# Layer 0 of a four-layer graph network: batches of 16 graphs, nodes packed into tiles by group

## Chip, cores and metric

One core of one Trainium2 chip. The metric is the time of one execution on the device, in microseconds (us), as the median of several runs.

## The reference, cut to what matters

128 graphs of 64 nodes with 256 features go through four layers, each with a residual and a layernorm. Layer 0 works on five groups of nodes (25, 9, 7, 6 and 6 of the first 25 nodes). Each group is two graph convolutions with its own weights, 256 to 512 to 256 features:

```python
GROUPS = [list(range(25)), [0,...,8], [0, 9,...,14], [6, 7, 8, 12, 13, 14], [3, 4, 5, 9, 10, 11]]
for g, idx in enumerate(GROUPS):
    x_g, adj_g = x[:, idx, :], adj[:, idx][:, :, idx]
    h     = relu(norm(adj_g) @ (x_g @ W1[g]) + b1[g])
    out_g = relu(norm(adj_g) @ (h @ W2[g]) + b2[g])
    fused[:, idx, :] += softmax(fusion_w)[g] * out_g
x = layernorm(x + fused)
# layer 1: a graph convolution; layer 2: a polynomial of the adjacency
# layer 3: five rounds of messages into a GRU: most of the matmuls, untouched by the change
```

Everything is float32.

## The kernel before

A chunk is 8 graphs, four pairs of 128 nodes. `back(c)` is layer 3 of chunk c; `front(c + 1)`, layers 0 to 2 of the next chunk, is laid between its steps (a step is what lies between two `yield`s), so that one has matmuls for TensorE while the other waits. Layer 0 puts four graphs' 25 nodes into a tile of 100 rows, two tiles per chunk, and keeps that shape for all five groups: nodes out of a group are zeros.

```python
NT = 2                      # layer-0 tiles of a chunk: four graphs, their first 25 nodes each
R = 4 * NJ                  # 100 rows
def front(c):
    # ... adjacency of the groups (A), transposed (AT); adjacency of the pairs
    # ... ag0 = first aggregation (pa), [features, nodes]
    for g in range(NG):
        hg = work.tile([128, 4, NT * R], F32, name="hg", bufs=2)
        if g:
            nc.gpsimd.memset(hg, 0.0)
        for e in range(4):                                  # ph: W1, only the group's nodes
            p = spread_like(psum("ph"), g)
            for k in range(2):
                nc.tensor.matmul(p, W1[:, g, k, e * 128 : (e + 1) * 128], part(ag0[:, k, g, :], g), ...)
            nc.scalar.activation(part(hg[:, e, :], g), p, AF.Relu, bias=b1[...])
        for t in range(NT):                                 # ps: W2, both full tiles for every group
            for e in range(4):
                nc.tensor.matmul(ps[:, t, :], hg[:, e, t * R : (t + 1) * R], W2[:, g, e, :], ...)
        nc.scalar.copy(s2, ps)
        yield
        for t in range(NT):                                 # po: second aggregation, nodes on partitions
            nc.tensor.matmul(po[:, t, :], AT[:, t, g, :], s2[:, t, :], start=True, stop=True)
        nc.vector.tensor_add(z, po, b2s[...])               # then relu, scale, fused += z
    for t in range(NT):                                     # pse: to the pairs' tiles
        for h in range(2):
            nc.tensor.matmul(p[:, h, :], sel[:, h, :], fused[:, t, :], start=True, stop=True)
        nc.vector.tensor_add(xt[...], p, xt[...])
    layernorm(xt)
    yield
    # ... layers 1 and 2, each ending in a layernorm on VectorE with a power on GpSimd
...
interleave(front(0), fold())
for c in range(NCH):
    if c + 1 < NCH:
        interleave(back(c), front(c + 1))
    else:
        interleave(back(c))
```

## Time and profile before

| | before |
|---|---|
| median of four runs | 2947.6 us (2946.25 to 2948.17) |
| profiled span | 2944.2 us |
| TensorE busy | 2784.7 us, 10712 instructions |
| start, until layer 3 of chunk 0 begins | 149.2 us |
| one chunk in the steady part | 177.4 us |
| last chunk | 134.4 us |

A change is judged by what it does to the start, to a steady chunk, and to the end. In a line of the timeline the columns are start, duration, engine, source line, operation, output and inputs by name, shapes (of a matmul: the stationary operand as rows*columns, then the moving one), count, and in brackets the idle time ahead with what ended it. `pT` is transposes, `pa`/`ph`/`ps`/`po`/`pse` are layer 0's stages (`pa` and `pT` serve other layers too), `pd` the projections of layers 1 and 2, `pn`/`pr`/`pz`/`pi` the GRU's gates and `pm` its messages. The distance from one group's start to the next, divided by its number of instructions, is called the pitch.

### The profile page before, as it was taken

The numbers are of one execution on the slowest core, as the hardware profiler recorded it, in microseconds if no ns is written. First come the engines' busy times: TensorE is split into PE (matmuls) and PEld (weight loads), VectorE is DVE, ScalarE is ACT, GpSimd is POOL, SyncE is SP. The second block draws the span as 40 slices with busy tenths as digits, with TensorE's granted clock in tenths as the row PEclk, the third lists the DMA queues.
The fourth block names the chain that finished last, engine by engine and source line by source line (L and its number), as shares of the span: only waits on it lengthen the run. The fifth ranks groups of instructions, "written<-read, shape, count | busy, mean of one in ns | idle before, by whom it ended". The sixth has DMA issues, their size and how long they took to land.

```text
span 2944.2 us, 27152 instructions
## 1 busy us (share of the span) xinstructions
PE 2784.7 (95%) x10712; PEld 1683.7 (57%) x10712; DVE 1197.2 (41%) x2503; ACT 813.1 (28%) x1443; POOL 182.5 (6%) x178
## 2 busy tenths in 40 slices
PE   4799999999999999999999999999999999999998
PEld 3656565565656656565565656556565565656644
DVE  3433425354352533525244352443525344252433
ACT  0132232322323222232322323223232222223222
POOL 2000100000010000100000000000100000000000
PEclk9899999999999999999999999999999999999999
DMA  5000000000000000000000000000000000000000
GB/s 170 2 4 2 18 1 13 7 2 18 1 17 3 2 18 1 20 0 7 13 2 18 0 17 4 2 18 1 17 3 2 17 1 15 1 8 0 1 7 8
DMA packets 38549, 34.01 MB, mean 12 GB/s; under 512 B 15082, under 2 KB 35762, under 8 KB 38422
## 3 DMA queue, kind: packets, MB, share of 16 engines
q1 hardware_dynamic: 34686, 23.69, 2.7%
q0 software_dynamic: 1504, 5.51, 0.6%
q10 hardware_dynamic: 2232, 3.08, 0.4%
q8 instruction: 85, 1.39, 0.2%
q14 instruction: 42, 0.34, 0.0%
HBM read 23.88 MB, written 8.39 MB: 11 GB/s over the span
## 4 chain that ended last, share of the span: by engine, by line
PE 79%; issue 9%; DVE 8%; POOL 2%; DMA 1%; ACT 1%; ACTq 0%; POOLq 0%; DVEq 0%; SPq 0%
PE ps L317 9%; PE pr L431 8%; PE pz L417 8%; PE pi L431 8%; PE pz L431 8%; PE pn L417 7%; PE pr L417 7%; PE ph L310 5%; PE pm L424 4%; PE po L325 2%; PE pa L226 2%; PE pa L294 2%; PE pT L453 2%; PE pd L369 2%; DVE st L192 1%
## 5 line engine op out<-in xcount | busy, mean ns | idle before, releaser
L436 DVE SCALAR_TENSOR_TENSOR r<-pn,bhh,r 128x512 f32<-128x512 f32 x160 | 120.1, 750 | 1094.4 <-ACT r L435 1094.4
L431 PE MATMUL pr<-agg,V 128*128 128x512 f32 x640 | 307.5, 603 | 0.0
L431 PE MATMUL pz<-agg,V 128*128 128x512 f32 x640 | 300.7, 592 | 0.0
L431 PE MATMUL pi<-agg,V 128*128 128x512 f32 x640 | 300.7, 592 | 0.0
L317 PE MATMUL ps<-W,hg 128*100 128x256 f32 x1280 | 292.7, 382 | 0.0
L435 ACT ACTIVATE r<-pr,brz 128x512 f32<-128x512 f32 x160 | 109.9, 687 | 610.8 <-PE pr L431 610.8
L417 PE MATMUL pn<-hn,WHH 128*128 128x512 f32 x512 | 253.2, 596 | 0.0
L417 PE MATMUL pr<-hn,WHH 128*128 128x512 f32 x512 | 243.6, 592 | 0.0
L317 PEld LDWEIGHTS ps<-W,hg 128*100 128x100 f32 x1280 | 210.1, 168 | 55.4
L417 PE MATMUL pz<-hn,WHH 128*128 128x512 f32 x512 | 240.6, 592 | 0.0
L428 ACT COPY agg<-pm 128x512 f32<-128x512 f32 x160 | 93.8, 586 | 494.8 <-PE pm L424 494.8
L431 PEld LDWEIGHTS pi<-agg,V 128*128 128x128 f32 x640 | 121.6, 190 | 153.1 <-issue 153.1
L431 PEld LDWEIGHTS pz<-agg,V 128*128 128x128 f32 x640 | 121.6, 190 | 153.1 <-issue 153.1
L439 ACT ACTIVATE n<-r,bih 128x512 f32<-128x512 f32 x160 | 115.5, 722 | 291.4 <-DVE r L437 291.4
L310 PEld LDWEIGHTS ph<-ag,W 128*128 128x128 f32 x1280 | 173.2, 191 | 26.4 <-issue 21.5
L431 PEld LDWEIGHTS pr<-agg,V 128*128 128x128 f32 x640 | 108.4, 189 | 124.1 <-issue 76.5
L310 PE MATMUL ph<-ag,W 128*128 128x48 f32 (+3 forms) x1280 | 170.9, 282 | 0.0
L417 PEld LDWEIGHTS pr<-hn,WHH 128*128 128x128 f32 x512 | 97.1, 190 | 122.6 <-issue 117.8
L417 PEld LDWEIGHTS pz<-hn,WHH 128*128 128x128 f32 x512 | 97.2, 190 | 116.1 <-issue 115.4
L197 POOL TENSOR_TENSOR rs<-ve,mhalf 128x4 f32<-128x4 f32 x64 | 64.4, 1007 | 1385.0 <-DVE ve L195 1344.5
L424 PEld LDWEIGHTS pm<-A,h 128*128 128x128 f32 x1024 | 124.4, 192 | 30.6 <-issue 30.6
L313 ACT ACTIVATE hg<-ph,b 128x48 f32<-128x48 f32 (+3 forms) x320 | 107.2, 347 | 95.2 <-PE ph L310 83.5
(109 smaller groups left out, 3264.9 us busy)
## 6 DMA issues: line engine op xcount, KB each, us to landing
xt<-in_x_dram SPq DMA_DIRECT2D x16, 512.0 KB
out_dram<-xt SPq DMA_DIRECT2D x16, 512.0 KB
x<-in_x_dram SPq DMA_DIRECT2D x128, 25.0 KB
W<-in_w_dram POOLq DMA_DIRECT2D x5, 512.0 KB, 8.1
W<-in_w_dram ACTq DMA_DIRECT2D x5, 512.0 KB
a<-in_adj_dram SPq DMA_DIRECT2D x128, 2.4 KB
a<-in_adj_dram SPq DMA_DIRECT2D x16, 128.0 KB
wl<-in_wlT_dram POOLq DMA_DIRECT2D x5, 256.0 KB, 5.5
```

What stands on the lines that cost most here:

```text
L197: nc.gpsimd.tensor_tensor(rs, ve, mhalf[:, :NP], ALU.pow)
L226: nc.tensor.matmul(p[:, q * 128 : (q + 1) * 128], src[:, q, k * 128 : (k + 1) * 128], m[:, q, :], start=True, stop=True)
L310: nc.tensor.matmul(p, W1[:, g, k, e * 128 : (e + 1) * 128], part(ag0[:, k, g, :], g), start=k == 0, stop=k == 1)
L313: nc.scalar.activation(part(hg[:, e, :], g), p, AF.Relu, bias=b1[:, g * 4 + e : g * 4 + e + 1])
L317: nc.tensor.matmul(ps[:, t, :], hg[:, e, t * R : (t + 1) * R], W2[:, g, e, :], start=e == 0, stop=e == 3)
L417: nc.tensor.matmul(p, WHH[:, k, q * 128 : (q + 1) * 128], hT[:, k, :], start=k == 0, stop=last and k == 1)
L424: nc.tensor.matmul(p[:, q * 128 : (q + 1) * 128], h[:, q, k * 128 : (k + 1) * 128], A01[:, q, :], start=True, stop=True,)
L428: nc.scalar.copy(agg[:, k, :], p)
L431: nc.tensor.matmul(p, V[:, l, k, q * 128 : (q + 1) * 128], agg[:, k, :], start=first and k == 0, stop=k == 1)
L435: nc.scalar.activation(r, pr, AF.Sigmoid, bias=brz[:, j : j + 1])
L436: nc.vector.scalar_tensor_tensor(r, pn, bhh[:, 4 + j : 5 + j], r, op0=ALU.add, op1=ALU.mult)
L439: nc.scalar.activation(n, r, AF.Tanh, bias=bih[:, 4 + j : 5 + j])
```

## The change

Its intent: no matmuls on zero rows. Layer 0 now takes 16 graphs at a time and packs each group's nodes alone into tiles: 4 tiles of 100 rows, 2 of 72, one of 112 and two of 96, nine per 16 graphs in place of twenty. Each packed tile is loaded directly. The second aggregation comes out with features on partitions, so that groups can be added by strided views along the free dimension, and `pse` becomes plain transposes. The 16 graphs' layer 0 is laid beside two chunks: ten steps at the end of an even chunk, the others at the beginning of the odd one. The core of the diff:

```diff
+SB = 16
+TILES = [(0, 4 * i, 4) for i in range(4)] + [(1, 8 * i, 8) for i in range(2)] + [(g, 0, SB) for g in (2, 3, 4)]
 ...
-            hg = work.tile([128, 4, NT * R], F32, name="hg", bufs=2)
-            if g:
-                nc.gpsimd.memset(hg, 0.0)
+            hg = work.tile([128, 4, w], F32, name="hg0" if g == 0 else "hg", bufs=1 if g == 0 else 2)
 ...
-            for t in range(NT):
-                nc.tensor.matmul(po[:, t, :], AT[:, t, g, :], s2[:, t, :], start=True, stop=True)
-            nc.vector.tensor_add(z, po, b2s[:, None, g * D : (g + 1) * D].to_broadcast([R, NT, D]))
+            for k in range(2):
+                for u, t in enumerate(ts):
+                    nc.tensor.matmul(p[:, ...], s2[u][:, k * 128 : (k + 1) * 128], AT[:r, t, :r], ...)
+                nc.scalar.activation(F[...] if g == 0 else z[...], p, AF.Relu, bias=gb2[...], scale=gw[...])
+            if g:
+                for f, n in RUNS[g]:
+                    nc.vector.tensor_add(F[:, :, :, f : f + n], F[:, :, :, f : f + n], z[...])
 ...
-                nc.tensor.matmul(p[:, h, :], sel[:, h, :], fused[:, t, :], start=True, stop=True)
+                    nc.tensor.transpose(p[:, h, k * 128 : (k + 1) * 128], F[:, k, b : b + 2, :]..., ident)
 ...
-    interleave(front(0), fold())
+    interleave(front0(0), fold())
+    interleave(front(0))
     for c in range(NCH):
-            interleave(back(c), front(c + 1))
+        if c % 2 == 0:
+            beside = both(front(c + 1), take(half, 10) if s < NS else ())   # half = front0(s), s = c // 2 + 1
+        else:
+            beside = both(half, front(c + 1)) if s < NS else ()
+        interleave(back(c), iter(beside))
```

Cut: the loads, the block masks, and buffers that shrank to make room.

## The prediction

> **What bounds the kernel now.** The page comes first, for its shares and its slices. Then the timeline of TensorE over a steady stretch of 200 us, its first 155 us and its last 210 us, and the whole chain of work for one chunk.
>
> ```profile
> PE 2784.7 (95%) x10712; PEld 1683.7 (57%) x10712; DVE 1197.2 (41%) x2503; ACT 813.1 (28%) x1443; POOL 182.5 (6%) x178
> ...
> PE   4799999999999999999999999999999999999998
> ...
> 40.88 1.91 PE L258 MATMUL pT<-ident,A 100*100 100x100 f32 x10 [40.88 <-DVE A L252]
> ...
> 126.13 3.62 PE L369 MATMUL pd<-L1W,ag 128*128 128x256 f32 x16
> 136.09 3.75 PE L226 MATMUL pa<-poly,xt 128*128 128x128 f32 x16 [6.34 <-DVE xt L199]
> 139.63 3.79 PE L385 MATMUL pd<-L2W,ag 128*128 128x256 f32 x16
> 149.19 2.10 PE L403 MATMUL pT<-ident,xt 128*128 128x128 f32 x8 [5.77 <-DVE xt L199]
> ...
> 1561.54 1.04 PE L453 MATMUL pT<-ident,hn 128*128 128x128 f32 x8
> 1567.65 2.10 PE L403 MATMUL pT<-ident,xt 128*128 128x128 f32 x8 [5.07 <-DVE xt L199]
> 1569.54 0.63 PE L424 MATMUL pm<-A,xt 128*128 128x128 f32 x2
> 1569.97 3.62 PE L417 MATMUL pn<-hT,WHH 128*128 128x512 f32 x4
> 1573.38 1.98 PE L417 MATMUL pr<-hT,WHH 128*128 128x512 f32 x4
> ...
> 1612.04 2.87 PE L310 MATMUL ph<-ag,W 128*128 128x200 f32 x16
> 1614.75 3.62 PE L317 MATMUL ps<-W,hg 128*100 128x256 f32 x16
> 1618.20 1.88 PE L417 MATMUL pn<-hn,WHH 128*128 128x512 f32 x4
> ...
> 1629.37 1.90 PE L310 MATMUL ph<-ag,W 128*128 128x72 f32 x16
> 1631.11 3.64 PE L317 MATMUL ps<-W,hg 128*100 128x256 f32 x16
> ...
> 1745.14 2.10 PE L403 MATMUL pT<-ident,xt 128*128 128x128 f32 x8 [5.07 <-DVE xt L199]
> ```
>
> TensorE is the bound. Between 1573 and 1745 us its groups start one at the end of the other, with one gap of 0.55 us. The only regular hole is at the boundary of chunks: `pT` of the next chunk (L403) waits 5.07 us for the layernorm of layer 2. It costs more than that: after it the four `pn` take 3.41 us to the start of `pr` instead of 1.72, and the eight `pT` 1.89 instead of 0.87. From the end of the last gate (`pz`, 1558.09) to 1573.38 are 15.29 us for 7.13 us of matmuls at full pace, so a boundary loses 8.2 us.
>
> The time of before adds up: the start until the first L403 at 149.19 us, 15 chunks of 177.4 us (to L403 at 2809.84), and a last chunk of 134.4 us without anything beside it; together 2944. The measured median is 3.4 us over the span.
>
> Starts of successive groups, not mean durations, give the price of a matmul. A float32 matmul is two instructions (640 of them for 320 calls on L431), a transpose one. One instruction costs 1.72/4 = 430 ns at 512 moving columns, 3.45/16 = 216 ns at 256, 2.71/16 = 169 ns at 200, 1.78/16 = 111 ns at 128, and still 109 ns at 72. So it is about (larger of moving and stationary columns)/1.2 + 2.5 ns. The ten 100x100 transposes take 0.86 us, 86 ns each, which fits.
>
> **What the Trainium skill says.** TensorE: Matmul & The Clock Gate, section "LDWEIGHTS (loading the stationary operand)": a load lasts by its columns, P/1.2 ns, whatever its rows. The trace agrees (109 ns floor with 128 stationary columns, 86 with 100), and it is why 48 or 72 moving columns cost what 128 do. Same page, section "Back-to-back issue gap": N/2.4 + 2.5 ns for an isolated matmul. Here float32 instructions take N/1.2 + 2.5; the measurement decides. Same page, "Part 1: The HAM clock gate": an idle window of about 3.4 us halves the clock, as long a busy one restores it. The trace agrees: the 5.07 us hole is followed by some 3 us of lost pace, the holes under 1 us by none. Trainium Kernel Development and Optimization, section "Performance Expectations": matmul busy time says little since matmuls overlap; here a group's mean duration (592 ns) indeed exceeds its pitch (430).
>
> **The change, part by part.** *Matmuls of layer 0, for 16 graphs.* Before, one chunk of 8: transposes 0.86; `pa` 8 x 419 ns = 3.35; `ph` 2.71 + 1.74 + 1.78 + 2 x 1.70 = 9.6 (groups 1 to 4 all at the floor); `ps` 80 x 216 ns = 17.3, all five groups on two full tiles of 100 rows though most rows are zero; `po` 20 x 216 ns = 4.3; `pse` 8 x 216 ns = 1.75. Sum 37.2, or 74.4 us for 16 graphs.
>
> After, the nine packed tiles (4 of 100 rows, 2 of 72, one of 112, 2 of 96), with the same pitch rule: transposes 9 x 96 ns = 0.9; `pa` 36 x 111 ns = 4.0; `ph` 16 x 336 (400 columns) + 16 x 122 (144) + 48 x 109 ns = 12.6; `ps` 72 x 216 ns = 15.6, for nine tiles in place of twenty; `po`, now features by nodes, 36 x 109 ns = 3.9; group sum 16 transposes x 109 ns = 1.7. Sum 38.6 us. Saved 35.8 us per 16 graphs, 286 us for all eight. The dropped zero memsets on GpSimd and the dropped bias additions on VectorE (687 ns each) lie beside TensorE and give nothing.
>
> *Boundaries of chunks.* The order of instructions of the changed kernel shows two kinds. After an even chunk, layers 1 and 2 of the next chunk were done in steps 1 to 7 of 17, and L0 work fills the end: no hole. After an odd chunk they take steps 11 to 17: after the last gate come only `pd` of layer 1, the last `pT` of layer 3, then `pa`, `pd` of layer 2 and the next chunk's transposes, each behind a chain on VectorE and GpSimd. That run stands alone in the start of before: `pd` at 126.13 to L403 at 149.19, 23.1 us, with holes of 6.34 and 5.77 us. Add 2.9 us of slow clock afterwards, subtract 9.55 us of full-pace work (3.45 + 0.87 + 1.78 + 3.45): 16.5 us lost. Two boundaries of before lost 16.4, so for the steady part the pair is even: half the holes, each twice as long. For the whole: before 15 x 8.2 = 123, after 7 x 16.5 = 116.
>
> *Small waits.* From the end of the last gate of a round to its `hn` transposed are 2.5 to 2.9 us (2.49 at 2836.32 in the last chunk). Before, long `ph` and `ps` groups covered that in most rounds; now the filler between rounds is often 1.7 us plus 0.44. I take six gaps of 0.4 us, 2.4 us per pair against 1.1.
>
> *Start.* The direct loads of the packed tiles take 30 issues in place of 16, plus two more large loads ahead of the constants. Before, one issue per 1.2 us (the 27th, `bhh`, at 33.45, landed 39.3, and the first transposes waited behind it in VectorE's order). `bhh` is now 43rd: about 16 later, first transposes near 57. The front of 16 graphs instead of 8 adds 1.5 us of matmuls and similar waits (72 us until the group sum, 71 before), then 37 us as before: first L403 at about 167.
>
> *Sum.* Steady work of a chunk outside layer 0 is 130.5 us (177.4 - 37.2 - 8.2 - 0.55, less 1.0 for switches between groups). A pair: 2 x 130.5 + 38.6 + 2 x 1.0 + 16.5 + 2.4 = 320.5. Total: 167 + 7 x 320.5 + 135 (chunk 14, with layers 1 and 2 of the last but no layer 0) + 131.5 (the last, without a cold start) = 2677, and 3.4 outside the span: 2680 us.
>
> **Rivals.** *The waits eat it.* If VectorE, in order and with GpSimd's powers (1.98 us each) in its way, delays the recurrent chain in each of the ten rounds of a pair by 1 us more, and odd boundaries lose 25 us, the sum is 2680 + 8 x 10 + 7 x 8.5 = 2820. Against it: VectorE is 41% busy and loses work. For it: layer-0 scaling with its wait on a power now sits between two rounds. *Only the even boundaries count.* If the odd boundary is no worse than one of before, the time is 2680 - 7 x 8.3 = 2622. For this I see little: the static order puts `pa` and `pd` after the last gate. *The saving is fiction.* If matmuls with 96 to 112 moving columns paid load and stream one after the other (109 + 90 ns), the 120 such instructions (`pa`, `po`, three of `ph`) would add 11 us per 16 graphs, 2770. Against it: 72 columns at 109 ns now. *Loads bind.* Many pieces of 4 to 12 bytes could make the packed tiles late; they are queued a chunk ahead and DMA is at 0 to 1 tenths after the start, so I give it 20 us at most, in the start.
>
> **Range and chances.** Matmul counts are exact and their pitch is measured; a 3% error of the saving is 9 us. The odd boundaries are known to 3 us each (21), the small waits to 2 us per pair (16), the start to 12. Together about 30, with more room above: 2640 to 2730. Faster by over 2% means under 2889, which only several failures at once would miss: 0.97; same 0.02, slower 0.01.
>
> **What would show it.** `ps` at 576 instructions in place of 1280, pitch 216 ns; `po` near 109 ns; `ph` at 400 columns near 336. No hole at even boundaries, at odd ones two of 5 to 7 us, one ahead of `pa` and one ahead of the next chunk's first transposes (L403 of before). Pairs of 320 us. The first of those transposes at 167 us. It is wrong if TensorE's gaps between rounds exceed 1 us, or a pair's length is off by over 8 us.

## The result, and the profile after

2669.3 us (median of four, 2668.16 to 2670.44) against 2947.6: ratio 0.9058, 95% interval 0.9045 to 0.9071. A ratio here is the mean time of one kernel's fast runs over that of the other's of the same rounds, so not quite the ratio of the medians. The prediction was 2680 with 2640 to 2730.

The page of the changed kernel, busy times and TensorE's slices:

```profile
PE 2491.1 (93%) x9408; PEld 1461.6 (55%) x9408; DVE 1077.2 (40%) x2394; ACT 712.9 (27%) x1219; POOL 108.2 (4%) x108
...
PE   2879999899989999899998999989999999989998
```

TensorE lost 294 us of busy time, more than the 276 us by which the span fell, and its slices now show eights between the nines: holes that were spread over every chunk stand together. TensorE's timeline of the changed kernel shows where, at the end of an even chunk and then of an odd one:

```profile
1271.42 1.93 PE L332 MATMUL po<-AT,s 100*128 100x100 f32 x16
1273.19 1.35 PE L500 MATMUL pT<-ident,hn 128*128 128x128 f32 x8
...
1276.34 3.62 PE L319 MATMUL ps<-W,hg 128*72 128x256 f32 x16
1279.79 1.04 PE L450 MATMUL pT<-ident,xt 128*128 128x128 f32 x8
...
1416.14 3.62 PE L416 MATMUL pd<-L1W,ag 128*128 128x256 f32 x16
1419.59 1.04 PE L500 MATMUL pT<-ident,hn 128*128 128x128 f32 x8
1426.04 3.75 PE L236 MATMUL pa<-poly,xt 128*128 128x128 f32 x16 [5.41 <-DVE xt L226]
1429.59 4.75 PE L432 MATMUL pd<-L2W,ag 128*128 128x256 f32 x16
1440.55 2.09 PE L450 MATMUL pT<-ident,xt 128*128 128x128 f32 x8 [6.21 <-DVE xt L226]
1442.43 1.92 PE L358 MATMUL pse<-ident,fusedT 128*128 128x128 f32 x8
1444.14 2.58 PE L464 MATMUL pn<-hT,WHH 128*128 128x512 f32 x4
1446.56 1.88 PE L464 MATMUL pr<-hT,WHH 128*128 128x512 f32 x4
```

At 1279.79 the next chunk's first transposes (L450, the place of L403 before) follow a `ps` without a hole. At the odd boundary there are two holes, each behind a layernorm (L226). From `pd` at 1416.14 to `pr` at 1446.56 are 30.42 us, for 13.0 us of work at full pace (3.45 + 0.87 + 1.78 + 3.45 + 0.87 + 0.87 + 1.72): 17.4 us lost. In the pair before this one the same stretch took 28.43 us, 15.4 lost.

Where the 276 us of the two spans come from:

| stretch | before | after | saved |
|---|---|---|---|
| start, until the first transposes of layer 3 | 149.2 | 164.25 | -15.1 |
| chunks 0 to 13 | 14 x 177.4 = 2483.6 | 7 pairs of 319.07 = 2233.5 | 250.1 |
| chunk 14 | 177.4 | 137.5 | 39.9 |
| last chunk | 134.4 | 132.9 | 1.5 |

A pair saved 2 x 177.4 - 319.07 = 35.7 us.

### The profile page after: what moved, and what is told of

Same layout as the page of the kernel before. It is cut to its first block, busy times and chain, and to the rows that moved or that the text cites. A ratio compares the mean times of both kernels' runs of the same rounds, so it can differ in the third digit from the quotient of the medians.

```text
span 2668.1 us, 23799 instructions
## 1 busy us (share of the span) xinstructions
PE 2491.1 (93%) x9408; PEld 1461.6 (55%) x9408; DVE 1077.2 (40%) x2394; ACT 712.9 (27%) x1219; POOL 108.2 (4%) x108
## 4 chain that ended last, share of the span: by engine, by line
PE 89%; DVE 5%; DMA 2%; ACT 1%; issue 1%; SPq 1%; POOL 1%; POOLq 0%; DVEq 0%; ACTq 0%
PE pr L478 11%; PE pz L478 10%; PE pi L478 10%; PE pz L464 10%; PE pn L464 10%; PE pr L464 10%; PE pm L471 5%; PE ph L305 4%; PE ps L319 3%; PE pa L236 3%; PE pT L500 2%; PE pd L416 2%; PE pd L432 2%; DMA xg<-in_x_dram 1%; PE pp L407 1%; PE po L332 1%
## 5 line engine op out<-in xcount | busy, mean ns | idle before, releaser
L464 PE MATMUL pn<-hn,WHH 128*128 128x512 f32 x512 | 247.8, 595 | 0.0
L478 PEld LDWEIGHTS pr<-agg,V 128*128 128x128 f32 x640 | 108.4, 189 | 124.2 <-issue 76.5
L319 PE MATMUL ps<-W,hg 128*100 128x256 f32 (+3 forms) x576 | 130.9, 379 | 0.0
L490 DVE TENSOR_TENSOR d<-hn,n 128x512 f32<-128x512 f32 x128 | 88.6, 692 | 100.8 <-ACT n L486 100.8
L491 DVE TENSOR_TENSOR d<-d,zg 128x512 f32<-128x512 f32 x160 | 110.5, 691 | 35.9 <-ACT zg L488 35.7
L471 PE MATMUL pm<-A,h 128*128 128x128 f32 x1024 | 124.6, 275 | 0.0
L484 DVE TENSOR_TENSOR r<-pi,r 128x512 f32<-128x512 f32 x160 | 110.7, 692 | 34.5 <-PE pi L478 34.3
```

The source lines that it names most:

```text
L319: nc.tensor.matmul(p[:r, h, :], hg[:, e, TOFF[t] - o : TOFF[t] - o + r], W2[:, g, e, :], start=e == 0, stop=e == 3,)
L464: nc.tensor.matmul(p, WHH[:, k, q * 128 : (q + 1) * 128], hT[:, k, :], start=k == 0, stop=last and k == 1)
L471: nc.tensor.matmul(p[:, q * 128 : (q + 1) * 128], h[:, q, k * 128 : (k + 1) * 128], A01[:, q, :], start=True, stop=True,)
L478: nc.tensor.matmul(p, V[:, l, k, q * 128 : (q + 1) * 128], agg[:, k, :], start=first and k == 0, stop=k == 1)
L484: nc.vector.tensor_add(r, pi, r)
L490: nc.vector.tensor_sub(d, hT[:, j, :], n)
```

## Experiments

The theory: TensorE's work in layer 0 lies wholly on the path, so each instruction less is worth its pitch; boundaries cost what their chains leave uncovered, twice as much at half as many places. Rivals: the relief of VectorE, ScalarE and GpSimd made the gain; the boundary holes are worth nothing in themselves; the turned orientation is a saving of its own. Nine kernels were run; eight gave the right result, one is wrong. The kernel before ran beside each of them with medians of 2947.2 to 2947.7 us, so that medians may be compared. The diffs are shortened, in places to pseudocode.

### 1. Double one stage of layer 0

```diff
-                    for e in range(4):
+                    for e in (0, 1, 2, 3, 0, 1, 2, 3):   # ps, in the changed kernel
```

> The changed kernel with every ps matmul (hidden layer to second weight matrix) done twice, the second round overwriting the first: 72 float32 matmuls = 144 instructions more per 16 graphs, nothing else on any engine; the result stays right. Theory (TensorE is the bound and layer 0's instructions lie on its path at 216 ns per pair of matmul instructions as counted in the prediction, 72 x 216 ns = 15.6 us per 16 graphs): 8 x 15.6 = 124 us more, about 2793 us (2775 to 2805). Rival (the gain of the change came from the lighter VectorE, ScalarE and GpSimd, and TensorE has slack in layer 0): less than 40 us more.

Measured: 2792.1 us (2791.09 to 2792.78), ratio to before 0.9475 (0.946 to 0.9489). That is 122.8 us over the changed kernel, where 124 were expected. The page and the group of `ps` with 100 rows, whose count doubled:

```profile
PE 2614.2 (94%) x9984; PEld 1557.9 (56%) x9984; DVE 1077.3 (39%) x2394; ACT 711.5 (25%) x1219; POOL 108.3 (4%) x108
...
L319 PE MATMUL ps<-W,hg 128*100 128x256 f32 x512 | 111.8, 379 | 0.0
```

The expectation calls the 72 additions matmuls; they are 36 matmuls of two instructions each, and its sum of 72 x 216 ns stands. Nothing else moved: VectorE's busy time is 1077.3 for 1077.2 us. 576 instructions more cost 122.8 us, 213 ns each. So a `ps` instruction is worth its pitch, and 704 fewer of them (1280 to 576) are worth some 152 us of the 278.

### 2. Give the other engines their old load back

```diff
+            if g:
+                for _ in range(3):
+                    nc.gpsimd.memset(hg, 0.0)
 ...  # after the activations of ph
+            for _ in range(2 if g == 0 else 4):
+                nc.vector.tensor_reduce(dv, hg, AX.XY, ALU.add)
+            for e in range(4):
+                for _ in range(2):
+                    nc.scalar.activation(da, hg[:, e, :96], AF.Relu)
```

> The changed kernel with dummy work on the other engines in layer 0, about as much as the change took away: per group 2 or 4 reductions on VectorE over the hidden tile, 8 small activations on ScalarE, 3 zero memsets of the hidden tile on GpSimd ahead of its use; TensorE's instructions and their order are the same, the result stays right. The change took 120 us from VectorE, 100 from ScalarE, 74 from GpSimd. Theory (all of it lay beside TensorE): 2669 to 2685 us with the busy times back near those of before. Rival (this relief was the gain): towards 2900.

Measured: 2668.2 us (2667.24 to 2669.98), 1.1 us under the changed kernel, with 111 us more on VectorE, 76 on ScalarE and 45 on GpSimd. Its page:

```profile
PE 2488.9 (93%) x9408; PEld 1459.9 (55%) x9408; DVE 1188.1 (45%) x2538; ACT 789.0 (30%) x1539; POOL 153.2 (6%) x204
```

VectorE got back 92% of what it had lost, the two others 76% and 61%. The time did not move, so a load of about that size beside layer 0 costs nothing, and the dropped memsets and bias additions gave nothing, as the prediction had it. (The dummy reductions and activations stand in their engines' order, but nothing reads them; only the memsets are ahead of work that TensorE waits for.)

### 3. Turn the second aggregation back

```diff
-                for u, t in enumerate(ts):      # 18 matmuls, [features, nodes], 72 to 112 columns moving
-                    nc.tensor.matmul(p[:, ...], s2[u][:, k * 128 : (k + 1) * 128], AT[:r, t, :r], ...)
+                for h in range(n):              # 9 matmuls, [nodes, features], 256 columns moving
+                    nc.tensor.matmul(p[:r, h, :], AT[:r, ts[u + h], :r], s2[u + h], ...)
```

> The changed kernel with the second aggregation turned back to nodes on partitions (the adjacency stationary, 256 feature columns moving): 9 float32 matmuls of 256 columns in place of 18 of 72 to 112 per 16 graphs; the result is wrong on purpose, because the group sum and the transposes after it are left as they are. Theory (a matmul instruction costs the larger of its moving and stationary columns, so 18 x 216 ns = 3.9 us against 36 x 109 ns = 3.9 us): 2664 to 2675, the same as the changed kernel. Rival (features on partitions is itself a saving on TensorE): 15 us or more slower.

Measured: 2669.4 us (2668.14 to 2670.09) against 2669.3; the result was wrong. Half the instructions at twice the length: the orientation is no saving on TensorE. Its use is that the group sum becomes strided additions.

### 4. Fill the boundaries of the kernel before

```diff
-    interleave(front(0), fold())
+    interleave(front_a(0), fold())              # front_a: layer 0, front_b: layers 1 and 2
+    interleave(front_b(0), front_a(1))
     for c in range(NCH):
-            interleave(back(c), front(c + 1))
+        interleave(back(c), both(front_b(c + 1), front_a(c + 2)))
```

> The kernel before with layer 0 done one chunk further ahead: beside chunk c stand layers 1 and 2 of chunk c+1 and then layer 0 of chunk c+2, so the chain behind the last layernorm has TensorE work beside it at each boundary; the same instructions in all. Theory (a boundary of before loses 8.1 to 8.2 us because nothing else is left to run): 15 x 8.1 = 122 us less, about 2825 us (2800 to 2840), no hole ahead of the first pT of layer 3 over 1 us. Rival (the holes are only the place where a slack shows that some other engine sets): the hole moves elsewhere and the time stays within 20 us of 2947.

Measured: 2870.7 us (2869.27 to 2877.41), ratio 0.9746 (0.9731 to 0.9761): 76.5 us less, not 122. TensorE's timeline at a boundary of this version shows what stayed:

```profile
1563.43 1.97 PE L314 MATMUL pse<-fused,sel 100*128 100x256 f32 x8 [2.87 <-DVE fused L310]
1565.23 1.04 PE L458 MATMUL pT<-ident,hn 128*128 128x128 f32 x8
1566.11 1.04 PE L408 MATMUL pT<-ident,xt 128*128 128x128 f32 x8
```

The 5.07 us hole ahead of the transposes (here L408) is gone, and a new one of 2.87 us stands a little earlier: layer 0 now ends there, and `pse` waits for the sum of the last group. Part of the wait changed its name. The boundary shown is one of the cheapest: behind the same hole the eight `pse` took from 1.96 to 3.75 us from chunk to chunk, and in one of the slowest the granted clock was 0.50 (350 to 353 us). So the experiment was repeated with `pse` and its layernorm moved to the next chunk.

```diff
+    def front_x(c):     # pse, residual and layernorm of layer 0
-        interleave(back(c), both(front_b(c + 1), front_a(c + 2)))
+        interleave(back(c), both(front_x(c + 1), front_b(c + 1), front_a(c + 2)))
```

> As the first filled version of before, but the selection matmuls pse and the layernorm of layer 0 are put off to the start of the next chunk, so that nothing at the end of a chunk waits for the group sum on VectorE. The first version took 2870.7 us and kept a hole of 2.87 us ahead of pse at each chunk's end. Theory (a boundary of before loses 8.1 us, of which 5.2 went with the first version and 2.87 stayed in that hole): 15 x 2.87 = 43 us less, about 2828 us (2815 to 2840), no hole over 1 us in the steady part. Rival (the remaining loss is something else at the boundary and the hole moves on): 2860 to 2870.

Measured: 2806.6 us (2806.57 to 2807.57), ratio 0.9522 (0.9509 to 0.9535). The boundary:

```profile
1520.01 1.11 PE L303 MATMUL po<-s,AT 100*100 100x256 f32 x4
1520.95 1.04 PE L413 MATMUL pT<-ident,xt 128*128 128x128 f32 x8
1522.22 1.98 PE L427 MATMUL pn<-hT,WHH 128*128 128x512 f32 x4 [0.24 <-ACT hT L414]
```

A steady chunk takes 169.26 us (1182.44 to 1520.95 are two of them) in place of 177.4: a boundary cost 8.14 us, which agrees with the prediction's 8.2. 15 x 8.14 = 122. The kernel gained 141; most of the other 19 us came in the start. There layer 0 of chunk 1 now fills the holes of chunk 0's chains: the first transposes of layer 3 are at 166.91, with 35.7 us of chunk 1's layer 0 already done (all but `pse`); less those, that is 131.2, against 149.2 before. The time is 21 us under the expected 2828 and outside its range. The profiles show two terms that the expectation had left out: the start gained 9 us more than in the first version (177.43 less 37.4 there), and a steady chunk fell by 4.4 us (173.7 to 169.3) and not by 2.87, since the slow clock behind the hole went too. (The profiled run of the first version was 6.7 us over its median, so the 4.4 is somewhat too large.)

### 5. Fill the boundaries of the changed kernel

```diff
-        if c % 2 == 0:   beside = front(c + 1), then ten steps of layer 0 of batch c // 2 + 1
-        else:            beside = the other steps, then front(c + 1)
+        if c % 2:        beside = front_x(c + 1), front_y(c + 1), then front_x(c + 2) and ten steps of layer 0 of batch c // 2 + 2
+        else:            beside = front_y(c + 1), then the other steps   # chunk 0: the whole of batch 1
```

`front_x` is here the group sum's transposes with the layernorm of layer 0, `front_y` is layers 1 and 2.

> The changed kernel with its layer-0 batch done half a pair earlier, so that 16 steps of layer-0 work stand beside the chains at the end of both chunks of a pair; the same instructions. Theory (each odd boundary loses 16.5 us by its two holes and the slow clock, each even one nothing): 7 x 16.5 = 115 us less, about 2554 us (2540 to 2580), with no hole of 5 to 7 us from chunk 1 on. Rival (the odd boundary's chain costs no more than one of before, 8.2 us): about 2612. Rival (the gain of the change came from elsewhere and the holes only move): 2640 to 2670.

Measured: 2566.1 us (2565.3 to 2567.06), ratio 0.8708 (0.8695 to 0.8721): 103 us under the changed kernel, by order alone. TensorE's timeline at both kinds of boundary:

```profile
1248.04 1.09 PE L454 MATMUL pT<-ident,xt 128*128 128x128 f32 x8 [0.30 <-ACT z L336]
...
1402.94 3.62 PE L319 MATMUL ps<-W,hg 128*72 128x256 f32 x16
1406.40 1.04 PE L454 MATMUL pT<-ident,xt 128*128 128x128 f32 x8
```

A pair takes 303.98 us (1102.42 to 1406.40), 15.1 less than the 319.07 of the changed kernel; the rule said 16.5. The rival that an odd boundary costs no more than one of before would have given 2612 and is out.

Now two kernels without boundary holes can be compared, which shows the matmuls alone. Layer 0's groups, from start to start in the timelines: 37.4 us for 8 graphs in the filled kernel before (transposes 0.86, `pa` 3.36, `ph` 9.6, `ps` 17.4, `po` 4.5, `pse` 1.7), 39.0 us for 16 in the filled changed one (0.9, 4.0, 12.6, 15.5, 4.3, 1.7). The prediction had 37.2 and 38.6. Per pair of chunks: 2 x 169.26 - 303.98 = 34.5 us of time saved, where 35.8 were predicted.

### 6. Packing or batch

Packed tiles, but 8 graphs at a time (six tiles per 8 graphs), with boundaries and start filled by the same order:

```diff
-SB = 16
+SB = 8
-TILES = [(0, 4 * i, 4) for i in range(4)] + [(1, 8 * i, 8) for i in range(2)] + [(g, 0, SB) for g in (2, 3, 4)]
+TILES = [(0, 4 * i, 4) for i in range(2)] + [(g, 0, SB) for g in (1, 2, 3, 4)]
```

> Packed tiles as in the changed kernel, but in batches of 8 graphs (six tiles per 8 graphs: 2 of group 0 and one of each other), with the chains at the ends of chunks filled; it splits the gain between the packing and the batch of 16. Layer 0 per 8 graphs by the prediction's rule: 6 transposes 0.6, 24 pa 2.7, ph 16 x 169 and 64 x 109 ns = 9.7, ps 48 x 216 = 10.4, 24 po 2.6, 8 transposes 0.9: 26.9 us, against 37.2 in the kernel before and 19.3 in the changed one. Theory: (37.2 - 26.9) x 16 = 165 us under the fully filled before (about 2828) = 2663, and 7.6 x 16 = 122 us over the filled changed kernel (2566) = 2688; so 2660 to 2690. Rival (packing is all, the batch of 16 is worth little): about 2570. Rival (the batch is all): about 2820.

Measured: 2715.6 us (2712.22 to 2717.97), ratio 0.9212 (0.9199 to 0.9224). Both rivals are out, but it lies 26 to 56 us above what I expected. A steady chunk takes 163.12 us; 169.26 - 10.3 = 158.96 was expected, 4.2 less. TensorE's timeline at the end of a chunk, and the stretches around it (stretch, its length, then busy time of TensorE, weight loads, VectorE, ScalarE and GpSimd, granted clock, DMA share, GB/s):

```profile
1622.85 1.93 PE L318 MATMUL ps<-W,hg 128*48 128x256 f32 x8
1628.55 3.42 PE L318 MATMUL ps<-W,hg 128*48 128x256 f32 x8
1632.43 0.64 PE L331 MATMUL po<-AT,s 48*128 48x48 f32 x4 [0.46 <-ACT s L323]
```

```profile
1625.00:1628.00 3.00, 2.74 (x24) 2.45 (x23) 2.59 (x11) 1.39 (x5) 0.00 (x0) 1.00 0.00 0
1628.00:1630.00 2.00, 2.00 (x10) 1.25 (x10) 1.63 (x9) 0.67 (x3) 0.19 (x1) 0.70 0.00 0
1630.00:1633.00 3.00, 2.54 (x9) 1.13 (x7) 1.38 (x4) 0.48 (x2) 0.82 (x1) 0.63 0.00 0
```

From start to start and at full clock, layer 0 sums to 28.7 us for 8 graphs, not 26.9; that its groups of four to eight short instructions change often is my reading, and no run isolated it. At a chunk's end `ph` and then `po` wait for ScalarE, 0.26 us (at 1626.64) and 0.46, 0.72 together. And in seven of the thirteen chunks from 324.61 to 2445.18 the clock fell, as in the second line: the same eight `ps` took 3.0 to 3.6 us and not 1.93. In three of the thirteen it fell at another place, behind layer 0's `pa`. The shortest chunks, with neither, take 161.82 us, so the slow clock is worth some 1.3 us per chunk in the mean. That is 3.8 of the 4.2 us; the other 0.4 I did not take apart.

### 7. The start

In the changed kernel's trace VectorE reads `fw` at 49.21, after 1.63 us of waiting, and the first packed transposes start at 52.82. The small constants were put at the head of another queue:

```diff
+    b2 = const(..., nc.scalar); bih = const(bihT, ..., nc.scalar); bhh = const(bhhT, ..., nc.scalar)
+    fw = spread(fusion_w, NG, "fw", eng=nc.scalar); cw = spread(conv_w, 4, "cw", eng=nc.scalar)
     b1 = const(b1T, [128, NG * 4], "b1", nc.scalar)
```

> The changed kernel with the five small constants that VectorE's first operations wait for (b2, bih, bhh, fw, cw) issued from ScalarE's queue ahead of b1 and W1, in place of behind the packed tiles' loads on SyncE's. Theory (the first packed transposes, at 52.8 us, wait for fw through VectorE's order, landed about 49.2): the first transposes move to 45 to 48 us, and the time falls by 4 to 8 us, to about 2663. Rival (the packed tiles themselves are late): no change within 1 us.

Measured: 2669.6 us (2667.89 to 2670.74), ratio 0.9056 (0.9044 to 0.9069), nothing gained. The first half of the theory held, the second did not. TensorE's and then VectorE's timeline of this version:

```profile
46.39 1.90 PE L279 MATMUL pT<-ident,A 112*112 112x112 f32 x9 [46.39 <-DVE A L259]
48.08 1.94 PE L197 MATMUL pf<-ih,wl 128*128 128x256 f32 x4
51.40 6.87 PE L197 MATMUL pf<-ih,wl 128*128 128x256 f32 x20 [1.37 <-DVE AT L280]
```

```profile
50.39 0.42 DVE L375 TENSOR_REDUCE rsum<-a 128x4 f32<-128x256 f32 x1 [3.01 <-DMA a<-in_adj_dram]
50.73 0.61 DVE L280 TENSOR_TENSOR AT<-pT,d0o 112x448 f32<-112x448 f32 x1
```

The transposes came 6.4 us earlier, but the next operation in VectorE's order was a sum over a later adjacency tile (L375) whose load had not landed. VectorE waited 3.01 us for it while the finished transposes stood behind it. TensorE then waits for VectorE's copies of the folded weights (`pf`) three times, 0.78, 2.27 and 1.02 us, where the changed kernel has one wait of 2.31. At the first `ps` the lead of 6.4 us has become a lag of 1.0 (96.02 against 94.98), and the first `pT` of layer 3 starts at 164.41 against 164.25. The Trainium skill, TensorE: Matmul & The Clock Gate, section "Architectural detail: the array is 16× 32×32, not 1× 128×128", says that VectorE's queue is strictly in order; these lines agree.

The last run filled the start as it had been filled in experiment 4:

```diff
-    interleave(front_y(0), front_x(1))
+    interleave(front_y(0), with_first(front_x(1), front0(1), 10))   # ten steps of batch 1's layer 0
```

> The changed kernel with filled boundaries, and the first ten steps of the second batch's layer 0 put beside layers 1 and 2 of chunk 0 in the start, as chunk 1's layer 0 stood there in the second filled version of before. In the filled changed kernel's start, between 127.6 and 165.2 us, TensorE has holes of 6.3, 0.8, 6.4 and 6.2 us, 19.7 together, and some 3 us at half pace behind them. Theory (the kernel is bound by TensorE's work, so these holes are worth their length): 2566 less 18 to 23, about 2545 us (2540 to 2552). Rival (the second batch's loads, which can only start when the first batch has read its features at about 70 us, come too late and hold VectorE in order): 2560 to 2575.

Measured: 2554.3 us (2553.03 to 2556.41), ratio 0.8664 (0.865 to 0.8679). That is 11.8 us less, and 18 to 23 were expected. Three holes are left in the stretch, in TensorE's timeline:

```profile
130.94 1.26 PE L279 MATMUL pT<-ident,A 112*112 112x112 f32 x8 [1.30 <-DVE xt L362]
135.96 0.44 PE L279 MATMUL pT<-ident,A 112*112 112x112 f32 x1 [3.76 <-DVE AT L397]
...
155.62 3.60 PE L236 MATMUL pa<-poly,xt 128*128 128x128 f32 x16 [3.99 <-DVE xt L226]
```

With one of 0.87 us they make 9.9 us, where 19.7 had been: half was filled, 9.8 us; the slow clock behind it may be the other 2. The expectation had counted all holes as filled. The rival of late loads is not seen in these lines: the waits are for VectorE's chains, and from 118 to 160 us VectorE itself waits for no load. This is the fastest version, 13.4% under the kernel before and 4.3% under the changed one.

### What the versions say together

| version | time, us | steady, us per chunk |
|---|---|---|
| before | 2947.6 | 177.4 |
| before, boundaries and start filled | 2806.6 | 169.3 |
| packed, batch of 8, filled | 2715.6 | 163.1 |
| changed kernel | 2669.3 | 159.5 |
| changed, boundaries filled | 2566.1 | 152.0 |
| changed, boundaries and start filled | 2554.3 | 152.0 |

With nothing left to wait for in the steady part, the change is worth 2806.6 - 2554.3 = 252 us: 91 for packing and 161 for the batch of 16. Of the 161, some 122 are by the pitch rule (7.6 us a chunk, as the expectation of experiment 6 works out), because at 8 graphs a tile of 48 to 72 rows costs what one of 96 to 112 does; the other 39 were not split further. In the steady part alone the extra is 163.1 - 152.0 - 7.6 = 3.5 us a chunk, for which experiment 6 gives its list.

## Why the prediction was right

*The pitch rule and the sum of layer 0 (35.8 us per 16 graphs).* Right: 35.8 by starts in the timelines (2 x 37.4 - 39.0), 35.7 by the length of a pair. `ps` stayed at 216 ns (3.45 us for 16, from 1276.34) and `po` came to 111 (1.77 for 16, from 1271.42). In the profile alone this could have been luck; doubling `ps` cost 122.8 of 124 us, which shows that these instructions are on the path.

*Boundaries a wash (123 against 116).* Right in size and kind. A boundary of before cost 8.14 us by removal (8.2 predicted), an odd one of after 15.4 or 17.4 in the trace and 15.1 by removal (16.5). Even ones have no hole. The terms inside came out a little otherwise: the chain from `pd` to the next transposes took 23.1 or 24.4 us (23.1 predicted), the slow clock behind it 1.8 or 2.5 (2.9).

*Nothing from the other engines.* Right: with most of their load back the time was 2668.2.

*Small waits (2.4 us per pair against 1.1).* Too large: in a pair TensorE waits 0.17 us once, and about five times the transposes of the state (L500) take 1.32 or 1.35 us in place of 1.04. That is some 1.6.

*Start (167).* 164.25. The term was nearly right and its reason partly wrong: I named `bhh` as the load that the first transposes wait for, and it was `fw`; the transposes came at 52.82 and not 57. Experiment 7 showed that this mattered little, since another load stood right behind it.

*Chunk 14 and the last (135 and 131.5).* 137.5 and 132.9, 3.9 us more together. The words "without a cold start" were wrong: at the end of chunk 14, with nothing beside it, TensorE waits 2.02 us for the state (to 2534.37), and the clock is 0.51 for the next 3.1 us. The last four transposes then take 0.87 us in place of 0.44, and the last chunk's first eight 1.70 in place of 0.87.

*The whole.* 2680 against 2669.3. A pair was 1.4 us shorter than predicted, 10 over seven pairs, the start 2.7 shorter, the end 3.9 longer, and the median 1.2 over the profiled span and not 3.4.

*Rivals.* Waits that eat the saving: excluded by experiment 2 and the length of a pair. (The 1.98 us that this rival gives for GpSimd's powers is that of layer 0's scaling; a layernorm's takes 1.01.) Only even boundaries count, 2622: excluded, an odd one is worth 15.1 us. The saving is fiction: excluded, the short matmuls have the pitch of the rule. Loads bind by at most 20 us in the start: the start did become 15.1 us longer, as the prediction's own sum had it (17.8).

What the prediction did not say: that the holes it counted as a wash could be had back by order alone. It showed 116 us for them; 103 were removed with the order alone changed: each compute engine's count of instructions is the same.

## What to carry to other kernels

Where one engine is full, price its instructions by the distance between starts, find which operand sets that price (moving or stationary columns), and pack until neither pads; the other engines' relief can be left out of the sum. When work that had covered the chains between stages is halved or regrouped, look at what is left to run at each boundary: here the waits grew to twice the length at half the places, and a different order was worth another 4%. A wait that is removed from an in-order engine may only uncover the next one in its queue, so look at that one before counting the gain.

## What the Trainium skill lacked or had wrong

- TensorE: Matmul & The Clock Gate, "Back-to-back issue gap", has no figure for float32; another page of the skill, FP8 and Floating Point Precision, says under "TensorE Precision Notes" that true float32 takes four passes. Here a float32 matmul is two instructions, each of N/1.2 + 2.5 ns at a granted clock of 1.00: 430 ns at 512 moving columns, 216 at 256, and at least 109 ns with 128 stationary columns. Two of them are 860 ns for 512 columns, four times N/2.4, so the four passes agree; the section gives neither this nor the two instructions. Layer 0's stages, summed from start to start, came out within 1.1% of this rule in the groups of the batch of 16 (39.0 for 38.6 us), and 7% over it in the short groups of the batch of 8 (28.7 for 26.9).
- Same page, "Part 1: The HAM clock gate": the rule of an idle window of about 3.4 us does not cover what these runs showed. After a hole of only 2.02 us (to 2534.37 in the changed kernel) the clock was 0.51; after one of 2.87 us in the first filled version of before it was 0.50 in one chunk (350 to 353 us) and 1.00 in another (from 1563.4). And in the batch of 8 it fell almost without a hole: to 0.70 and 0.63 from 1628 to 1633 us, though TensorE had been idle for only 0.26 us in the three before, and to 0.54 from 1393.3 to 1397.0, though TensorE had been busy all through the 3.3 before. What ran ahead of the first were transposes and matmuls with 48 stationary or 48 moving columns, ahead of the second 24 `pa` with 100 moving columns; that low use of the array causes it is my guess, and no run isolated it.
- Same page and section: a busy window of about 3.4 us is said to restore the clock. Behind the 6.2 us hole at an odd boundary the stretch from `pT` to `pr` took 5.3 or 6.0 us for 3.46 of work, which is 3.7 or 5.1 us at half pace (granted clock 0.50 from 1440 to 1445 us). At the boundary of before, 1567.65 to 1573.38, it was half pace for all of 5.7 us. So the return took from 1.1 to 1.7 such windows. The page says that it varies with the phase of a free-running window, but gives no such range.
